# Ranks of scores counted by ScalarE's signs beside VectorE, and three inner products later in their turn

## The chip, the cores and the metric

The kernel runs on one core of one Trainium2 chip. The core has five engines with a queue of instructions each: TensorE (PE in the profile, its weight loads PEld), VectorE (DVE), ScalarE (ACT), GpSimd (POOL) and SyncE (SP), which here only issues DMAs. An engine takes its own instructions strictly in order; between engines there are semaphores. The metric is the device time of one launch in microseconds (us), the median of several runs.

## The reference, cut to what matters

Six layers of a decoder work on x, 16 sequences of 128 tokens by 256 features. Each is followed by a residual and a layernorm: a mixture of experts with ternary weights, a cross attention with a distance bias, an int4 feed-forward layer, **a state-space model with a memory pool**, a masked cross attention, and a feed-forward layer of chosen experts. The change lies in the fourth:

```python
xn = _rmsnorm(x, norm_w)
z, xBC, dt = split(xn @ in_proj_w)            # 512, 512+128+128, 8 columns
dt = softplus(dt + dt_bias)
xBC = silu(conv4(xBC))                        # 4 taps along the tokens
xs, Bm, Cm = split(xBC)
y = _ssd(xs * dt, dt * A, Bm, Cm) + xs * D    # decayed, causal (Cm Bm^T) xs
y = _rmsnorm(y * silu(z), ssm_norm_w) @ out_proj_w
scores = sigmoid(relu(y @ scorer_w1) @ scorer_w2)
summaries = y @ summ_w
# a scan over all 2048 tokens: a token with score > 0.5 is written to one of
# 50 slots; when they are full it replaces the lowest if it is higher
pool, count = scan(step, summaries, scores)
retrieved = softmax(y @ q_w @ (pool @ k_w).T / 4) @ (pool @ v_w)
y = y + sigmoid([y, retrieved] @ gate_w) * retrieved
```

The kernel has no scan. It gives every token a rank: the number of tokens with a higher score, plus the equal ones that came earlier. The 50 tokens with the lowest ranks are the pool.

## The kernel before, in words

One sequence is one block of 128 tokens, on the 128 partitions; there are NB = 16 blocks, n = 0 to 15, in four groups g of four. `stage3` calls `ssm` and then `memory`. Both have a written-out order: in `ssm` the order of the program text is the order on every engine, in `memory` this holds for PE alone. Before that, `stage2` (cross attention, L915 to L1003, and the int4 layer) runs under a scheduler that orders the instructions by need.

`ssm` has a **prologue** for the first group, and then 18 **turns** n = 0 to 17. In turn n the block n is finished, block n+1 is prepared, block n−1 is written back, and two of the six column sets of the next group's convolution are made. The small functions, with their lines and engines:

- `convolved` L1294 (PE, in_proj), `taps` L1296 and L1303 (ACT, DVE: four taps), `tanh` L1309 (ACT) and `curved` L1312 (DVE) make cT, the silu of the convolution, of one column set of a group. Silu is u·(1+tanh u) with u half the argument, so the weights carry a 0.5: L1631 scales the z half of in_proj on DVE, in the prologue.
- `decay` L1387 (POOL) and `decayed` L1392, L1393 (ACT) make the decay matrix mT of a block. `inner(n+1)` L1399 to L1407 makes B·C of the block (PE), masks it (bc, DVE), transposes xs (PE L1404) and scales it by dt (xd, DVE). `joined` L1411 (POOL) multiplies mT by bc.
- `gate` L1423 (PE), `gate_tanh` L1429 (ACT), `gated` L1435 (DVE) make silu(z) for two blocks.
- `outer(n)` L1443 (PE) multiplies mT and xd into ps_y, `skipped` L1452 (DVE) adds xs·D, `passed` L1458 (POOL) multiplies by silu(z): yf.
- `measured` L1463 (ACT, square) and `added` L1469 (POOL) prepare the RMS norm, `projected` L1476 (PE) is out_proj, `summed` L1481 (PE), L1483 (DVE, ys) and L1485 (POOL, yrs) make the factor, `scaled` L1490 (ACT, y) and L1491 (DVE, x), `kept` L1496 (PE) and an ACT copy make yT.
- The norm's weight is multiplied into out_proj once: four instructions L1646 on DVE in the prologue.
- After each group: `remembered(g)` L1504, L1506, L1512, L1513, L1516 and L1520, L1521 (query, summaries, scores of 512 tokens), in turns 7, 11, 13 and after the last. `lined` L1528 and `ranked` L1536 to L1542 bring the scores of the group to all partitions as `row` and to columns as `key`, in turns 8, 12, 14 and after the last.
- `counted(g)` is a generator on DVE: three instructions for equal scores (L1551, L1554, L1555), then for each block b up to 4g+3 one comparison of its 128 keys with the group's 512 row entries (L1560, summed as it goes), and one more with all earlier blocks (L1564) if b is in the group. Two of its steps are taken at the end of every turn from 11 on, and all that is left after the last turn. The sums land in columns of `larger`.
- `others(k)` copies k banks of the fifth layer's keys and values, which PE makes meanwhile (L1905, L1912), out of PSUM (kv, ACT L1583) and stores them (SP, L1584). Each third bank uses the one ps_y buffer.

At the start of `memory` PE makes twelve further parts of the fifth layer's keys and values (`meanwhile(12)`: L1958 and L1978, each copied to a ring by ACT at L1961 and L1982), with two PSUM buffers between them. DVE counts meanwhile, and then reduces `larger` to `rank` (L1758). With `rank`, a matrix `pick` of tokens by slots is made, and PE collects the summaries with it (L1770).

Of the kernel before, what the change touches and what calls it, by code (L numbers as in the profile page):

```python
# [19 lines left out]
P = 128  # L20
NB = 16
# [1201 lines left out]
def stage3(K, w, kv_banks, between):  # L1223

    tc, nc = K.tc, K.nc
    with ExitStack() as ctx:
        keep = ctx.enter_context(tc.tile_pool(name="s3_keep", bufs=1, side="right"))


        m = SimpleNamespace(pool=keep)  # L1230
        m.yT = K.new(keep, [P, KD, NB * P], F32, "yT")
        m.qT = K.new(keep, [SUM, NB * P], F32, "qT")
        m.summ = K.new(keep, [P, NB, SUM], F32, "summ")
        m.score = K.new(keep, [P, NB], F32, "score")
        m.key = K.new(keep, [P, NB], F32, "key")
        m.row = K.new(keep, [P, NB, P], F32, "row")
        m.larger = K.new(keep, [P, 6, NB], F32, "larger")
        nc.vector.memset(m.larger, 0.0)
        ssm(K, w, m, kv_banks)
        memory(K, w, m, between())  # L1240


def ssm(K, w, m, kv_banks):
# [6 lines left out]
    with ExitStack() as ctx:  # L1250
# [178 lines left out]
        def gate_tanh():  # L1429
            to, pz = gates[0]  # L1430
            nc.scalar.activation(to, pz, AF.Tanh)

# [45 lines left out]
        def summed(n):  # L1478
# [3 lines left out]
            t = K.new(small, [P, 1], F32, "ys")  # L1482
            nc.vector.tensor_scalar(t, pn, 1.0 / DI, 1e-5, ALU.mult, ALU.add)  # L1483
            s.yrs = K.new(small, [P, 1], F32, "yrs")
# [15 lines left out]
        def remembered(g):  # L1500
# [19 lines left out]
            nc.scalar.activation(score, psc, AF.Tanh, scale=0.5)  # L1520
            nc.vector.tensor_scalar(score, score, 1.0, 0.5, ALU.add, ALU.mult)  # L1521


        def lined(g):
# [3 lines left out]
            nc.vector.tensor_tensor(  # L1528
                diag, K.ident.unsqueeze(1).to_broadcast(W), m.score[:, mine].unsqueeze(2).to_broadcast(W), ALU.mult,
            )  # L1530

        def ranked(g):
# [6 lines left out]
            pkey = K.new(ps, [P, 4], F32, "ps_s", bufs=1)  # L1539
            nc.tensor.matmul(pkey, K.ident, m.score[:, mine], start=True, stop=True)  # L1540
            nc.scalar.copy(m.row[:, mine, :], prow)
            nc.vector.tensor_copy(m.key[:, mine], pkey)  # L1542

        def counted(g):
            mine = slice(4 * g, 4 * g + 4)
            W = [P, 4, P]
            rowf = m.row.rearrange("p b t -> p (b t)")
            junk = K.new(m.pool, [P, NB * P], BF16, "junk")
            end = 512 * g + 512
            own = junk[:, :512].rearrange("p (b t) -> p b t", t=P)  # L1550
            nc.vector.tensor_tensor(  # L1551
                own, m.row[:, mine, :], m.key[:, mine].unsqueeze(2).to_broadcast(W), ALU.is_equal,
            )
            nc.vector.tensor_tensor(own, own, K.lower.unsqueeze(1).to_broadcast(W), ALU.mult)  # L1554
            nc.vector.tensor_reduce(m.larger[:, 5, mine], own, AX.X, ALU.add)  # L1555
            yield
            for b in range(4 * g + 4):
                s = m.key[:, b:b + 1]
                at = max(b * P, 512 * g)
# [3 lines left out]
                if b >= max(4 * g, 1):  # L1563
# [3 lines left out]
                    )  # L1567
                if b % 4 == 3:
                    yield

# [14 lines left out]


        squared(0)
        normed(0)
# [41 lines left out]
        curved(0, 1)  # L1630
        nc.vector.tensor_scalar(w.inp[:, :, :DI], w.inp[:, :, :DI], 0.5, None, ALU.mult)  # L1631
        taps(0, 2)
# [11 lines left out]
        gate(1)  # L1644
        for k in range(DI // P):
            nc.vector.tensor_scalar(w.out[:, k, :], w.out[:, k, :], w.ssm_norm[:, k:k + 1], None, ALU.mult)  # L1646
        others(2)
        curved(0, 3)
        inner(0)
        joined(0)  # L1650
        order, late, counts = (4, 5, 0, 1, 2, 3), None, iter(())
        for n in range(NB + 2):
# [17 lines left out]
            elif gating:  # L1670
# [3 lines left out]
                gate_tanh()  # L1674
            if late is not None and i == 3:
                curved(*late)
                late = None
            if new:
                inner(n + 1)
            if late is not None:  # L1680
                curved(*late)
            if new:
                decayed(n + 1)
# [14 lines left out]
            if old:  # L1698
                summed(n - 1)
            if n == NB:  # L1700
                others(4)
            if now:
# [14 lines left out]
            if n in (7, 11, 13):  # L1717
                remembered({7: 0, 11: 1, 13: 2}[n])
            if n in (8, 12, 14):
                k = {8: 0, 12: 1, 14: 2}[n]  # L1720
                ranked(k)
                counts = counted(k)
            if n > 10:
                next(counts, None)
                next(counts, None)
        remembered(3)
        all_of(counts)
        lined(3)
        ranked(3)
        all_of(counted(3))  # L1730
        assert next(banks, None) is None and not gates


def memory(K, w, m, kv):
    tc, nc = K.tc, K.nc
    x = K.x
    with ExitStack() as ctx:
# [19 lines left out]
        rank = K.new(one, [P, NB], F32, "rank")  # L1757
        nc.vector.tensor_reduce(rank, m.larger.rearrange("p k b -> p b k"), AX.X, ALU.add)  # L1758
        pick = K.new(one, [P, NB, SLOTS], F32, "pick")
        ppool = K.new(ps, [SUM, SLOTS], F32, "ps_s")  # L1760
# [822 lines left out]
```

## Time and profile before

| | |
|---|---|
| three runs | 1406.60, 1406.64, 1410.62 us; median 1406.64 us |
| the profiled execution | 1407.58 us |
| its span, first to last instruction | 1405.9 us, 1.68 us less |
| mean granted clock of TensorE | 0.950 |
| busy shares | PE 88%, DVE 60%, ACT 47%, POOL 35% |
| prologue of `ssm` | about 410 to 456 us of the span |
| turns 0 to 11 | about 456 to 590 us |
| turns 12 to 17, and the last ranks' row | about 590 to 662 us |
| twelve parts for the fifth layer, beside the last counts | 662 to 685 us |

Times in the text are microseconds from the start of the span. An entry of the timeline is: start, duration, engine, line, what is written from what, shape; in square brackets the idle time before it, and what ended it. A row of a chain has start, duration, engine, tile and line of each step of the work that ended last; a row of waits has what waits, for what, the sum of the waits, how often, and the longest.

### The profile page before, as it was taken

The page shows a single profiled execution, that of the slowest core. Times are in us where ns is not written, and L with a number is a line of the kernel's source. Part 1 is how long each engine was busy: PE and PEld are TensorE (multiplying, and loading weights), DVE is VectorE, ACT ScalarE, POOL GpSimd, SP SyncE. Part 2 cuts the span into 40 slices and gives each one's busy share as a digit, 9 for nine tenths or more (in the row PEclk, how much of TensorE's full clock was granted, in tenths as well). Part 3 has the DMA queues.
Part 4 walks back from the last instruction along what each step waited for, and adds up shares of the span by engine and source line. Part 5 has one row for each costly group of instructions (what it writes and reads, how often), then busy time and mean ns, then how long its engine had stood idle before and what let it go on. Part 6 is the DMA issues. An engine that isn't in the chain of part 4 may idle for free.

```text
span 1405.9 us, 19207 instructions
## 1 busy us (share of the span) xinstructions
PE 1239.4 (88%) x6743; PEld 851.2 (61%) x6743; DVE 842.1 (60%) x1791; ACT 658.1 (47%) x1689; POOL 489.8 (35%) x643
## 2 busy tenths in 40 slices
PE   3678887889978798878998999999889999999995
PEld 1455444667654576655655788877777655666553
DVE  7799978999958887876644565667333111211115
ACT  5779865789955655422223566654522111111110
POOL 4256557678851776641043233222202000000003
PEclk9899988999999999867999999999999999999998
DMA  8458324111112211102000221211005232232002
GB/s 300 143 172 291 120 80 84 17 39 31 32 53 69 72 49 46 45 1 83 8 0 1 69 83 61 76 61 46 1 8 188 69 99 62 85 105 91 21 9 75
DMA packets 63120, 103.53 MB, mean 74 GB/s; under 512 B 11920, under 2 KB 41712, under 8 KB 62768
## 3 DMA queue, kind: packets, MB, share of 16 engines
q1 hardware_dynamic: 60848, 96.76, 20.7%
q0 software_dynamic: 2176, 5.55, 1.9%
q8 instruction: 53, 0.87, 0.3%
q14 instruction: 43, 0.35, 0.1%
HBM read 81.74 MB, written 16.35 MB: 70 GB/s over the span
## 4 chain that ended last, share of the span: by engine, by line
PE 53%; DVE 29%; ACT 6%; POOL 5%; issue 4%; DMA 2%; another core or an unknown queue 0%; SPq 0%; DVEq 0%; POOLq 0%; ACTq 0%
PE ps_y L2413 7%; PE ps_m L2402 7%; PE ps_g L2402 7%; PE ps_m L1958 4%; DVE acc L1303 3%; PE ps_m L2089 3%; PE ps_t L2080 2%; ACT s L2060 2%; DVE cT L1312 2%; PE ps_m L1978 2%; DVE s L915 1%; DVE m L2054 1%; DVE s L2050 1%; PE ps_s L2047 1%; PE ps_t L2069 1%
## 5 line engine op out<-in xcount | busy, mean ns | idle before, releaser
L2407 DVE TENSOR_TENSOR h<-h,ps_m 128x512 f32<-128x512 f32 x60 | 41.3, 688 | 228.3 <-PE ps_m L2402 228.3
L82 POOL TENSOR_SCALAR ln_t<-ln_mv 128x1 f32<-128x1 f32 (+1 forms) x84 | 16.6, 197 | 448.7 <-DVE ln_mv L90 308.3
L2060 ACT ACTIVATE s<-s,m 128x128 f32<-128x128 f32 x256 | 99.4, 390 | 69.1 <-DVE m L2054 69.1
L2406 ACT ACTIVATE h<-ps_g 128x512 f32<-128x512 f32 x60 | 35.8, 597 | 171.0 <-PE ps_g L2402 171.0
L2402 PE MATMUL ps_g<-xin,w 128*128 128x512 f32 x224 | 106.2, 592 | 0.0
L2402 PE MATMUL ps_m<-xin,w 128*128 128x512 f32 x224 | 105.3, 592 | 0.0
L2413 PE MATMUL ps_y<-w,h 128*128 128x256 f32 x448 | 97.8, 379 | 0.0
L2413 PEld LDWEIGHTS ps_y<-w,h 128*128 128x128 f32 x448 | 85.1, 190 | 14.6 <-issue 3.3
L2064 POOL TENSOR_TENSOR s<-s,t 128x1024 f32<-128x1024 f32 x32 | 60.7, 1898 | 90.7 <-DVE t L2063 90.7
L927 ACT ACTIVATE s<-s,m 128x128 f32<-128x128 f32 x256 | 83.2, 394 | 11.7 <-DVE m L922 11.7
L2402 PEld LDWEIGHTS ps_m<-xin,w 128*128 128x128 f32 x224 | 42.5, 190 | 51.4 <-issue 50.2
L2402 PEld LDWEIGHTS ps_g<-xin,w 128*128 128x128 f32 x224 | 42.0, 190 | 46.4 <-issue 45.0
L1958 PE MATMUL ps_m<-xT,half 128*128 128x256 f32 x256 | 62.6, 389 | 2.6 <-DVE qT L1963 1.9
L2050 DVE TENSOR_TENSOR s<-ps_s,hide 128x1024 f32<-128x1024 f32 x32 | 39.2, 1224 | 35.9 <-PE ps_s L2047 35.9
L2414 ACT COPY y<-ps_y 128x256 f32<-128x256 f32 x30 | 11.2, 372 | 104.7 <-PE ps_y L2413 66.2
L2089 PE MATMUL ps_m<-half,oT 128*128 128x256 f32 x256 | 59.3, 385 | 0.0
L1303 DVE SCALAR_TENSOR_TENSOR acc<-ps_m,l1a_conv_w,acc 128x508 f32<-128x508 f32 (+2 forms) x72 | 53.3, 740 | 3.4 <-ACT acc L1296 1.7
L1958 PEld LDWEIGHTS ps_m<-xT,half 128*128 128x128 f32 x256 | 47.4, 194 | 9.2 <-DVE qT L1963 2.3
L2089 PEld LDWEIGHTS ps_m<-half,oT 128*128 128x128 f32 x256 | 47.4, 190 | 7.5
L83 POOL TENSOR_TENSOR ln_rs<-ln_t,mhalf 128x1 f32<-128x1 f32 (+1 forms) x84 | 48.7, 580 | 7.0
L1411 POOL TENSOR_TENSOR mT<-mT,bc 128x1024 f32<-128x1024 f32 x16 | 37.7, 2357 | 36.3 <-DVE bc L1401 16.9
L2060 ACT ACTIVATION_READ_ACCUMULATOR s<-s,m 128x1 f32 x256 | 48.2, 188 | 0.0
(514 smaller groups left out, 3111.2 us busy)
## 6 DMA issues: line engine op xcount, KB each, us to landing
w<-in_w_gate_dram SPq DMA_DIRECT2D x9, 1024.0 KB
csb<-cs_dram SPq DMA_DIRECT2D x16, 512.0 KB
w<-in_l1f_gateT_dram SPq DMA_DIRECT2D x14, 512.0 KB
w<-in_l1f_upT_dram SPq DMA_DIRECT2D x14, 512.0 KB
w<-in_l1f_downT_dram SPq DMA_DIRECT2D x14, 512.0 KB
k<-kv SPq DMA_DIRECT2D x20, 256.0 KB
v<-kv SPq DMA_DIRECT2D x20, 256.0 KB
ring<-k SPq DMA_DIRECT2D x10, 512.0 KB
```

The source lines that it names most:

```text
L83: return self.nc.gpsimd.tensor_tensor(out, t, self.mhalf[: out.shape[0], :n], ALU.pow)
L927: nc.scalar.activation(at, at, AF.Exp, bias=m[h][:, i:i + 1])
L1303: nc.vector.scalar_tensor_tensor(accv[:, :, j:], pcv[:, :, :P - j], w.conv[:, c, TAPS - 1 - j:TAPS - j], accv[:, :, j:], ALU.mult, ALU.add,)
L1411: nc.gpsimd.tensor_tensor(st[n].mT, st[n].mT, bc, ALU.mult)
L1958: nc.tensor.matmul(pq[:, j, :], wt[k][:, at], src[:, k, :], start=(k == 0), stop=(k == KD - 1))
L2050: nc.vector.tensor_tensor(half(b, j), pss.rearrange("p r c k -> p (r c) k"), hide.unsqueeze(1).to_broadcast([P, 8, P]), ALU.add,)
L2060: nc.scalar.activation(at, at, AF.Exp, bias=m[j][:, i:i + 1], accum_out=t[j][:, i:i + 1])
L2064: nc.gpsimd.tensor_tensor(half(b, j), half(b, j), t[j].unsqueeze(2).to_broadcast([P, 8, P]), ALU.mult)
L2089: nc.tensor.matmul(py[b], oT[b][:, c, :], w.o[c // 4][:, c % 4, :], start=(c == 0), stop=(c == NC - 1))
L2402: nc.tensor.matmul(ps[:, j, :], m[k][:, c * P:(c + 1) * P], self.r.xin[:, k, e, cols], start=(k == 0), stop=(k == KD - 1),)
L2407: nc.vector.tensor_tensor(h, h, pu, ALU.mult)
L2413: nc.tensor.matmul(pd, rows(c), w.down[c // 4][:, c % 4, :], start=(c == 0), stop=(c == FI // P - 1))
```

## The change

- **Scalings.** L1631 goes; the gate's tanh halves its input instead (`scale=0.5`). What this leaves, a factor of two in yf, is taken back in `ys` (0.25 for 1) and in out_proj (times 0.5). The four instructions on out_proj go from DVE (L1646) to POOL; they depend only on loaded weights, and stand on POOL's queue in `stage2`, between the two L989 at 329.79 and 330.98. The clearing of `larger` (and of a new `signs`) goes from DVE to POOL, before the prologue.
- **Inner products.** In turns 3, 7 and 11, the last of a group, `inner(n+1)`, `decayed(n+1)` and `joined(n+1)` come after `projected`, `gated` and `summed` of the turn, not before. They use the next group's cT, whose last two `curved` fall into this turn.
- **Banks for the fifth layer.** One bank fewer is copied at the end of the prologue, one each in turns 12, 14 and 15, between `summed` and `outer`, and two instead of four in turn 16.
- **Counts.** Scores are turned into whole units of 2^-24 (`units`, one small DVE instruction per group); row and key are made of these. Two small DVE instructions per group make −key∓0.5, the biases `above` and `below`. A count can then be made by ACT as well: the sign of row + bias, summed as it goes into `signs`; a count is (sum of signs + number)/2, and a POOL instruction of one column adds the half number. The turns change too: turn 11 does group 0 on DVE as before; turn 12 counts nothing (before: equals of group 1 and four blocks); turn 13 equals of group 1, DVE blocks 4 and 5, ACT 0 and 1; turn 14 DVE 6, 7, ACT 2, 3; turn 15 equals of group 2, DVE 8, 9, ACT 0 to 3; turn 16 DVE 10, 11, ACT 4 to 7. For group 3, after the turns, ACT takes blocks 0 to 5, 14 and 15 (ten passes: six of 512 elements, then 256, 1792, 128 and 1920), DVE 6 to 13. These ACT passes stand on ACT's queue ahead of all copies to the ring in `memory`. In `memory` one reduction and one small combination on DVE join `signs` to `rank`.

```diff
-        nc.vector.memset(m.larger, 0.0)
+        m.units, m.below, m.above = (K.new(keep, [P, NB], F32, t) for t in ("units", "below", "above"))
+        m.larger = K.new(keep, [P, 7, NB], F32, "larger")
+        nc.gpsimd.memset(m.larger, 0.0)
+        m.signs = K.new(keep, [P, 5, NB], F32, "signs")
+        nc.gpsimd.memset(m.signs, 0.0)
...
-            nc.scalar.activation(to, pz, AF.Tanh)
+            nc.scalar.activation(to, pz, AF.Tanh, scale=0.5)
...
-            nc.vector.tensor_scalar(t, pn, 1.0 / DI, 1e-5, ALU.mult, ALU.add)
+            nc.vector.tensor_scalar(t, pn, 0.25 / DI, 1e-5, ALU.mult, ALU.add)
...
+            nc.vector.tensor_scalar(m.units[:, 4 * g:4 * g + 4], score, 0.5, 2.0 ** 24, ALU.subtract, ALU.mult)
...
             nc.vector.tensor_copy(m.key[:, mine], pkey)
+            nc.vector.tensor_scalar(m.above[:, mine], m.key[:, mine], -1.0, -0.5, ALU.mult, ALU.add)
+            nc.vector.tensor_scalar(m.below[:, mine], m.key[:, mine], -1.0, 0.5, ALU.mult, ALU.add)
...
+            def by_scalar(b):
+                junk = held["junk"]
+                at = max(b * P, 512 * g)
+                nc.scalar.activation(
+                    junk[:, at:end], rowf[:, at:end], AF.Sign, bias=m.above[:, b:b + 1],
+                    accum_out=m.signs[:, g, b:b + 1],
+                )
+                n = end - at
+                if b >= max(4 * g, 1):
+                    nc.scalar.activation(
+                        junk[:, :b * P], rowf[:, :b * P], AF.Sign, bias=m.below[:, b:b + 1],
+                        accum_out=m.signs[:, 4, b:b + 1],
+                    )
+                    n += b * P
+                nc.gpsimd.tensor_scalar(m.larger[:, 6, b:b + 1], m.larger[:, 6, b:b + 1], 0.5 * n, None, ALU.add)
...
+        for k in range(DI // P):
+            nc.gpsimd.tensor_scalar(w.out[:, k, :], w.out[:, k, :], w.ssm_norm[:, k:k + 1], 0.5, ALU.mult, ALU.mult)
...
-        nc.vector.tensor_scalar(w.inp[:, :, :DI], w.inp[:, :, :DI], 0.5, None, ALU.mult)
...
-        for k in range(DI // P):
-            nc.vector.tensor_scalar(w.out[:, k, :], w.out[:, k, :], w.ssm_norm[:, k:k + 1], None, ALU.mult)
-        others(2)
+        others(1)
...
+        counts = {
+            11: ((equals0, None), (vector0, 0, 1, 2, 3)), 13: ((equals1, None), (vector1, 4, 5), (scalar1, 0, 1)),
+            14: ((vector1, 6, 7), (scalar1, 2, 3)), 15: ((equals2, None), (vector2, 8, 9), (scalar2, 0, 1, 2, 3)),
+            16: ((vector2, 10, 11), (scalar2, 4, 5, 6, 7)),
+        }
...
-            if late is not None and i == 3:
-                curved(*late)
-                late = None
-            if new:
+            if new and i < 3:
                 inner(n + 1)
             if late is not None:
                 curved(*late)
-            if new:
+            if new and i < 3:
                 decayed(n + 1)
                 joined(n + 1)
...
+            if new and i == 3:
+                inner(n + 1)
+                decayed(n + 1)
+                joined(n + 1)
+            if n in (12, 14, 15):
+                others(1)
             if n == NB:
-                others(4)
+                others(2)
...
+        for k in range(8):
+            by_scalar((0, 1, 2, 3, 4, 5, 14, 15)[k])
+            by_vector((6, 7, 8, 9, 10, 11, 12, 13)[k])
...
+        signs = K.new(one, [P, NB], F32, "signs_all")
+        nc.vector.tensor_reduce(signs, m.signs.rearrange("p k b -> p b k"), AX.X, ALU.add)
+        nc.vector.scalar_tensor_tensor(rank, signs, 0.5, rank, ALU.mult, ALU.add)
```

## The prediction

> **What bounds the kernel now.** I read the page first, for the shares of the chain that ended last. It stands for the whole span.
>
> ```profile
> span 1405.9 us, 19207 instructions
> PE 53%; DVE 29%; ACT 6%; POOL 5%; issue 4%; DMA 2%; another core or an unknown queue 0%; SPq 0%; DVEq 0%; POOLq 0%; ACTq 0%
> ```
>
> The change touches some 250 us of it, the state-space layer. So I cut that into stages by windows (columns: bounds, length, busy time of PE, PEld, DVE, ACT, POOL with counts, granted clock of PE, DMA).
>
> ```profile
> 410.00:456.00 46.00, 40.78 (x151) 24.29 (x152) 32.23 (x73) 27.70 (x66) 7.79 (x11) 0.93 0.18 64
> 456.00:590.00 134.00, 117.63 (x645) 86.44 (x644) 107.48 (x198) 77.28 (x125) 93.03 (x73) 0.96 0.17 58
> 590.00:662.00 72.00, 55.24 (x223) 37.61 (x224) 48.85 (x120) 17.92 (x35) 24.52 (x22) 0.74 0.04 15
> 662.00:690.00 28.00, 27.49 (x125) 19.73 (x125) 23.68 (x55) 7.63 (x13) 0.00 (x0) 0.94 0.23 76
> ```
>
> The turns to 590 are PE's, at nearly full clock. From 590 to 662 nothing is full and the clock is 0.74: there waits decide. From 662 PE is full; DVE counts below it. The waits of PE between 415 and 665, and the timeline of turn 3, say where PE stands still.
>
> ```profile
> PE ps_m L1404 <- DVE cT L1312: 12.4, 4, 4.2
> PE ps_s L1481 <- DVE bc L1401: 5.2, 3, 2.2
> ```
>
> ```profile
> 489.70 1.59 POOL L1469 TENSOR_TENSOR sq<-sq 128x256 f32<-128x256 f32 x2
> 491.02 0.33 PE L1404 MATMUL ps_m<-ident,cT 128*128 128x128 f32 x1 [4.21 <-DVE cT L1312]
> 491.19 3.50 PE L1476 MATMUL ps_o<-l1a_out_proj,yf 128*128 128x256 f32 x8
> 494.82 1.09 PE L1443 MATMUL ps_y<-mT,xd 128*64 128x128 f32 x16
> 497.16 1.27 POOL L1458 TENSOR_TENSOR yf<-yf,sz 128x512 f32<-128x512 f32 x1 [1.45 <-DVE yf L1452]
> ```
>
> PE waits 4.21 us for the last curved set, and then out_proj's eight matmuls take 3.50 us, where at full clock the same eight take 1.89. The chain of waits has them in all three turns, and in turn 13 the products after the fourth group's scores:
>
> ```profile
> 454.05 1.05 DVE l1a_out_proj L1646 x4
> 491.35 3.33 PE ps_o L1476 x8
> 532.06 3.08 PE ps_o L1476 x8
> 575.91 2.58 PE ps_o L1476 x8
> 608.30 3.78 PE ps_m L1504 x4
> 661.80 8.94 PE ps_m L1958 x32
> ```
>
> **The change part by part.** Base is the profiled execution, 1407.58 us (span 1405.9 and 1.68 around it), 0.94 above the median 1406.64.
>
> *Stage 2, POOL.* Four products of 128x256 on POOL before L989 at 330.98. They read one large input. The nearest rows are a POOL memset (L823, 128x2560 in 2.22 us, so 0.22 for 256 columns, 0.35 with some 0.13 of start, an estimate from L82's 0.19 for one column) and L989, two inputs of the same shape, 0.73. Four: 1.4 to 2.9, I take the middle, 2.2. Their weights landed near 328.3, before POOL is there (330.5), so no DMA is waited for. POOL had 0.46 idle there; behind stands L989, L935 and the factor ln_rs at 334.95, which DVE took at 335.63, 0.7 later. So 2.2−0.46−0.7 = **+1.1** (0 to +2.4); DVE is busy 14.35 of the 15 us from 325 to 340 and may be late enough itself to hide it all, hence the 0; +2.4 is the upper price, 2.9, with the idle alone taken off. The two memsets lie in an idle of POOL of 2.4 us: 0.
>
> *Prologue.* DVE's chain loses L1631 (0.60) and L1646 (1.05), 1.65. Curved(0,3) at 455.02 then waits for its tanh, done at 454.2: it can start 1.4 to 1.5 earlier. **−1.5** (−1.3 to −1.65). One bank less there (ACT 0.59, a store of SP): ACT is 60% busy, 0.
>
> *Turns 3, 7, 11.* L1476 moves into the idle before 491.02: its yf is there at 487.9, it ends about 489.8 at the full clock that PE still has. What is late next is POOL's sq, at 491.29, for L1481. Then L1399, L1404 and L1443, about 492.5 in place of 494.82; yf on DVE 493.7. But POOL is behind too: ys and yrs, then L1411 (bc now later, 2.34) ends at about 495.05; L1458 behind it starts there, for 497.16: −2.1. Turn 7: 537.81 to 535.75. Turn 11: L1504 from 580.61 to 578.5. **−6.3** (0 to −6.6; three sums of 2.1). DVE had 2.25 idle before ys in turn 3, so it can follow; 0 is the end where the next turns are DVE's (80% busy) and not PE's.
>
> *Turn 12.* 6.77 us of counts (597.41 to 604.18) leave DVE ahead of bc(14). bc was waited for by PE's L1481 (part of the 5.2 us) and POOL's L1411 (2.97). Next late are PE's gate products and the tanh (sz), mT's Exp on ACT to 603.27, then L1411, yrs, y, yT, L1504, which stood at 608.30 and comes at 605.6 to 607.0: **−2.0** (−1.0 to −2.7).
>
> *Clock in turn 13.* L1504, L1512 and L1516 took 8.9 us at clock 0.50 (608.30 to 617.2); in turn 11 the three took 4.6 at full clock (580.61 to 585.2), after the turns 6.4 (651.47 to 657.86) at 0.73 to 0.79. PE idled 1.60 and 1.94 just before, and both waits shrink, so I take the row in the middle: 8.9−6.4 = **−2.5** (0 to −4.3).
>
> *Turns 13 to 17.* DVE loses group 1's and 2's blocks to ACT: two, two, four and four passes. An ACT pass of 512 is 0.62 (L1463, the same shape) plus its accumulator read of 0.19, less overlap: 0.72. In turns 15 and 16 four each, 2.9, stand ahead of sq(15) and yT(15) on ACT's queue, and a bank's copy (0.59) ahead of outer(15), which needs ps_y: PE's L1912 (2.00) and the copy put +1.65 there; SP's store is behind it and nobody waits for that. Against it: ys in turn 16 came behind DVE's counts at 646.66, and two banks fewer stand there. Row by row 34.35 in place of 34.05 from the third scores to L1504 of the last group: **+0.3** (−1.5 to +2.5). Units and biases, three DVE instructions of 0.15 per group, on the chain in the last: **+0.2** (0 to +0.5). POOL's columns of 0.2 stand behind nothing that is late.
>
> *Last ranks.* After the row copy (661.16 to 661.75) ACT has ten passes: six of 0.72, then 0.50, 1.82, 0.39, 1.93 (0.86 ns an element, from L1392's 128x1024 of 1.05, and 0.18): 8.95 (7.95 to 10.8). Counted from the row copy's start, they run from 0.75 to 9.7. Only then ACT copies PE's first finished part, till 10.3. A part is eight matmuls of L1958, 1.73 each in the later four (6.91) and 3.8 for the first of the early four (8.94−3×1.73). PE has two PSUM buffers: it does two parts, from 0.64 to 6.15, and waits for that copy, 4.15 us idle. Ten parts at 1.72 are left, till 27.5; after 4.21 us of idle in turn 3 eight matmuls were 1.6 slow, here the first part was 2.0 slow, so 1.8 more: 29.3, where L1770 stood at 23.86 (685.02−661.16). **+5.5** (+2.7, cheap passes and no half clock, to +7.7, dear passes). DVE's counts fall from 20 to 10 us there, and that is worth 0: they lay beside PE's parts, which end at 684.5. What the parts cost PE is the same, so nothing behind them is shorter.
>
> Sum: +1.1−1.5−6.3−2.0−2.5+0.3+0.2+5.5 = **−5.2**, so 1402.4 as a profiled execution, and 0.94 less, 1401.4, as a median.
>
> A rule of the Trainium skill speaks against the tail. "TensorE: Matmul & The Clock Gate", Part 1, says that the clock is halved after one idle window of about 3.4 us and comes back after about 3.4 us of sustained work. Turn 3 agrees (4.21 us idle, then 3.50 for 1.89). Turn 13 does not quite: the rows show 0.50 from 608 to 620 with PE busy 3.7 to 4.0 of every 4. By the page alone the tail's second idle costs about 1.7, an estimate, near the 1.8 that I took from the row; by turn 13's row the whole tail could run at half.
>
> **The rivals.**
>
> R1, slower: after its idle PE stays at half clock, as from 608 to 620. A part at half is +1.8. The sum holds one; with 6 more the change is −5.2+10.8 = +5.6, and from there R1 decides; all nine give +11.0, 1417.6. For it: turn 13. Against it: before, the parts began at 0.50 and were at 0.62 within two, 0.94 over the stage; PE is dense there.
>
> R2, the move does nothing: turns 4 and 8 start no earlier, since POOL (L1411, L1387, 93 of 134 us) or DVE carries them. −5.2+6.3 = +1.1: 1407.7, no change. For it: L1411 is later than before against L1399. Against: PE's 117.6 of 134 is the fullest, and DVE has 4.6 us idle in turn 3 in four pieces.
>
> R3, better: full clock in turn 13 (−1.8 more), POOL's products hidden in stage 2 (−1.1), the passes at 7.95 and no half clock after them (−2.0): −10.1, 1396.5. For it: clock 1.00 after 646.
>
> R4, stage 2 loses more: POOL's delay goes round between DVE and POOL once more, +2 to +3: 1403.9, no change. For it: DVE's 14.35 of 15 us there. Against: later idles of POOL.
>
> **How the numbers follow.** A change under 0.3%, 4.2 us, is about what a measurement of this kernel cannot tell from none; faster begins below 1402.4. The main case has 0.44 and its own range 1398.5 to 1404.7, from the half clock in turn 13 and the passes; 0.27 of it falls under 1402.4 and 0.17 over it. R3 0.20, faster. R2 0.13 and R4 0.08, same. R1 0.10, slower; 0.05 for ACT's passes holding up turns 15 and 16 by more than their bound, slower. Faster 0.47, same 0.38, slower 0.15. The range 1394 to 1410 leaves out R1 and the last case, and 0.05 below it.
>
> **What would show it.** Right: L1476 in turns 3, 7 and 11 at 1.9 us, and PE waiting there for POOL's sq; L1443 at 492.5 less the prologue's gain; no DVE count between turns 12's L1491 and bc; ten ACT passes after the last row copy, then a wait of PE on ACT of about 4 us at the third part, and DVE idle long before L1770. Wrong: turns 4 and 8 starting their L1443 no earlier than before, once the prologue's gain is taken off (R2); PE's clock at 0.5 for 10 us in the parts (R1); a sign pass far from 0.72, or a load of ACT's table beside it; PE waiting for yT(15) in turn 17 for more than 3 us.

## The result, and the profile after

In the first comparison the changed kernel took 1408.13 us (median of 20 runs, 1402.73 to 1412.90), the kernel before 1407.93 us (20 runs, 1405.85 to 1410.62): ratio 0.9998, 95% interval 0.9987 to 1.0009. In absolute terms that is between 1.8 us less and 1.3 us more. The change made no difference that this measurement can tell; 1401.4 us was forecast, 5.2 less than before. The profiled execution took 1408.86 us.

To find where the 5.2 us went I cut both profiled executions at the same events, read off the timeline: the 11th, 16th and 32nd row of stage 2's x (L1003), the yf of blocks 2 and 11 (L1458, now L1461), the third group's scores (L1521, now L1524), the last row copy (L1541, now L1546), the start of the sum over slots (L1770, now L1810), the first x row that the fourth layer's layernorm writes behind it (L93, near 710 us), and the end of the last output row. Each number is the us from one event to the next.

| stretch | before | after | difference | forecast for it |
|---|---|---|---|---|
| start to x row 11 of stage 2 | 327.08 | 328.97 | +1.9 | 0, nothing changed there |
| x row 11 to 16, GpSimd's four products | 21.56 | 22.75 | +1.2 | +1.1 |
| x row 16 to 32 | 63.01 | 63.02 | 0.0 | 0 |
| to yf(2): prologue, first turns | 74.96 | 72.62 | −2.3 | −1.5 |
| to yf(11): turns 3 to 11 | 95.05 | 91.01 | −4.0 | −6.3 |
| to the third scores: turns 12, 13 | 35.76 | 31.70 | −4.1 | −4.5 |
| to the last row copy: turns 14 to 17 | 43.74 | 45.50 | +1.8 | +0.5 |
| to the sum over slots: last ranks | 23.86 | 31.45 | +7.6 | +5.5 |
| to x at 710 | 24.69 | 23.16 | −1.5 | 0 |
| to the end of the last output row | 693.35 | 694.09 | +0.7 | 0 |

The stretches from row 11 to 710 add up to −1.4 us. The first and last rows hold none of the change; a profile of the same changed kernel taken later has 331.06 in the first. So single stretches, which repeat within some 0.1 us where TensorE's clock does the same, say more than one profile's total.

The page and the windows of the same four stages, of the changed kernel, answer to those shown of before:

```profile
span 1407.2 us, 19229 instructions
...
PE 52%; DVE 29%; ACT 8%; POOL 6%; issue 4%; DMA 1%; another core or an unknown queue 0%; SPq 0%; DVEq 0%; ACTq 0%; POOLq 0%
```

```profile
410.00:456.00 46.00, 39.25 (x151) 23.31 (x151) 32.04 (x71) 26.58 (x65) 9.38 (x16) 0.96 0.19 59
456.00:590.00 134.00, 119.23 (x650) 85.19 (x651) 111.75 (x214) 78.14 (x127) 94.47 (x74) 0.97 0.16 54
590.00:662.00 72.00, 52.85 (x239) 33.64 (x237) 43.16 (x102) 33.06 (x75) 26.62 (x42) 0.83 0.08 26
662.00:690.00 28.00, 23.43 (x99) 16.65 (x100) 9.09 (x23) 10.84 (x18) 0.00 (x0) 0.88 0.23 75
```

From 590 to 662 VectorE is busy 43.16 us and not 48.85, ScalarE 33.06 and not 17.92, and TensorE's clock is 0.83 and not 0.74. These windows stand at the same microseconds in both kernels, though, and the changed kernel makes its last row copy at 655.57 and not at 661.16, so 6.4 us of its last ranks lie in the third window. From that copy to the sum over slots the windows are, of the kernel before and then of the changed one:

```profile
661.16:685.02 23.86, 22.89 (x81) 16.46 (x82) 23.16 (x52) 7.51 (x13) 0.00 (x0) 0.91 0.27 89
```

```profile
655.57:687.02 31.45, 25.74 (x82) 18.24 (x82) 14.82 (x36) 16.46 (x32) 0.00 (x0) 0.84 0.20 67
```

The change did what it says: VectorE's work falls from 23.16 to 14.82 us and ScalarE's rises from 7.51 to 16.46. But TensorE, which fills the stretch, now stands still for 5.7 us and not 1.0. In the chain ScalarE has 8% and not 6. Where TensorE stands still is in its waits, here of the changed kernel from 415 to 690 (what waits, for what, sum, times, longest):

```profile
PE ps_o L1479 <- POOL yf L1461: 10.1, 9, 2.3
PE ps_m L1507 <- ACT yT L1500: 6.0, 2, 3.1
PE ps_s L1484 <- DVE bc L1404: 5.7, 2, 3.0
PE ps_s L1484 <- POOL sq L1472: 5.6, 6, 1.4
PE ps_m L1998 <- ACT ring L2001: 5.3, 1, 5.3
PE ps_m L1407 <- DVE cT L1315: 2.0, 1, 2.0
```

The waits for the last curved set in turns 3, 7 and 11 (11.9 of the 12.4 us before) are gone, as intended; the one of 2.0 that is left lies in the prologue. The waits for yf (7.2 us before) and for sq are what replaced them. Those for yT are one of 2.9 in turn 13 and one of 3.1 in turn 17, and the wait for the ring copy is the stop of the last ranks. The timeline of the changed kernel shows the last ranks:

```profile
655.57 0.59 ACT L1546 COPY row<-ps_m 128x512 f32<-128x512 f32 x1 [3.30 <-PE ps_m L1541]
...
656.18 0.72 ACT L1582 ACTIVATE csb<-row,above 128x512 bf16<-128x512 f32 x1
...
657.03 0.72 ACT L1582 ACTIVATE csb<-row,above 128x512 bf16<-128x512 f32 x1
...
663.93 1.88 ACT L1588 ACTIVATE csb<-row,below 128x1920 bf16<-128x1920 f32 x1
...
665.93 1.07 ACT L2001 COPY ring<-ps_m 128x512 f32<-128x512 f32 x2
...
666.57 6.74 PE L1998 MATMUL ps_m<-ctxT,l1x_W_k 128*128 128x256 f32 x16 [5.25 <-ACT ring L2001]
...
673.15 7.03 PE L2018 MATMUL ps_m<-l1x_W_v,ctxT 128*128 128x512 f32 x16
...
687.02 2.07 PE L1810 MATMUL ps_s<-pick,summ 128*64 128x50 f32 x32
```

The passes follow each other every 0.85 us, the first ring copy stands behind all ten, PE waits 5.25 us for it, and then needs 6.74 us for two parts (16 matmuls) that take 3.5 at full clock. The windows of the changed kernel have the clock in the column before the DMA share:

```profile
662.00:666.00 4.00, 0.00 (x0) 0.00 (x0) 3.89 (x9) 3.97 (x7) 0.00 (x0) 0.99 0.00 0
666.00:672.00 6.00, 5.43 (x13) 4.35 (x14) 4.99 (x14) 1.59 (x3) 0.00 (x0) 0.50 0.85 282
672.00:687.00 15.00, 15.00 (x53) 9.85 (x51) 0.00 (x0) 4.69 (x8) 0.00 (x0) 0.98 0.08 27
```

Four microseconds without a matmul (the wait began at 661.3), 6.8 at half clock, then full clock. The trace also records each change of the granted clock. In the 17 traces of this case it is 1.00 or 0.50 and nothing else, and the time between two changes is 3.41 us or a whole multiple of it; here it was 0.50 from 665.9 to 672.7. A mean such as 0.74 is a mixture of the two. Below, a stay is such a time at half clock.

### The profile page after: what moved, and what is told of

Read it like the earlier page. It is cut to its first block, busy times and chain, and to the rows that moved or that the text cites. A ratio compares the mean times of both kernels' runs of the same rounds, so it can differ in the third digit from the quotient of the medians.

```text
span 1407.2 us, 19229 instructions
## 1 busy us (share of the span) xinstructions
PE 1234.8 (88%) x6731; PEld 843.2 (60%) x6743; DVE 824.7 (59%) x1755; ACT 676.4 (48%) x1733; POOL 495.5 (35%) x669
## 4 chain that ended last, share of the span: by engine, by line
PE 52%; DVE 29%; ACT 8%; POOL 6%; issue 4%; DMA 1%; another core or an unknown queue 0%; SPq 0%; DVEq 0%; ACTq 0%; POOLq 0%
PE ps_y L2453 7%; PE ps_m L2442 7%; PE ps_g L2442 7%; PE ps_m L1998 4%; DVE acc L1306 2%; PE ps_m L2129 2%; ACT s L2100 2%; PE ps_t L2120 2%; PE ps_m L2018 2%; DVE cT L1315 1%; DVE s L915 1%; DVE m L2094 1%; DVE s L2090 1%; PE ps_t L2109 1%; PE ps_s L2087 1%
## 5 line engine op out<-in xcount | busy, mean ns | idle before, releaser
L927 ACT ACTIVATE s<-s,m 128x128 f32<-128x128 f32 x256 | 83.3, 395 | 11.7 <-DVE m L922 11.7
```

The source lines that it names most:

```text
L927: nc.scalar.activation(at, at, AF.Exp, bias=m[h][:, i:i + 1])
```

## The experiments

Every run is set against runs of the kernel before on the same chip, whose median was 1406.8, 1408.5, 1407.1 and 1404.5 us in the four groups of runs. So ratios are compared, not microseconds: 0.001 is 1.4 us. A ratio below is to the kernel before, with its 95% interval; the changed kernel's own is 0.9998. The stretches of the table above, taken in the profiles of ten of these runs:

| kernel | prologue | turns 3-11 | turns 12, 13 | turns 14-17 | last ranks | to 710 |
|---|---|---|---|---|---|---|
| before | 74.96 | 95.05 | 35.76 | 43.74 | 23.86 | 24.69 |
| changed | 72.62 | 91.01 | 31.70 | 45.50 | 31.45 | 23.16 |
| counts on VectorE | 72.00 | 92.58 | 34.52 | 48.29 | 24.82 | 26.42 |
| four passes | 72.67 | 90.99 | 31.68 | 45.49 | 22.90 | 24.80 |
| copies between | 71.92 | 92.41 | 29.11 | 44.05 | 23.29 | 24.75 |
| yT first | 72.62 | 90.95 | 33.29 | 39.50 | 30.12 | 24.80 |
| both repairs, second time | 71.90 | 92.21 | 33.30 | 39.53 | 23.42 | 24.82 |
| move undone | 71.85 | 95.62 | 31.66 | 48.28 | 30.01 | 24.75 |
| move undone, second time | 72.97 | 95.05 | 32.08 | 43.93 | 30.12 | 24.75 |
| before, with the move | 73.91 | 91.31 | 34.71 | 43.65 | 23.86 | 24.70 |

A stretch has the same number in many kernels and jumps by 1 to 3 us in others, where nothing of it was edited (turns 14 to 17 with the counts on VectorE: 48.29 and not 45.50, in the same order). Each of these jumps that I followed up was TensorE at half clock for a few microseconds more or less. So one profile shows where a wait is; what it is worth needs many runs.

### The changed kernel again

> The changed kernel as it is, beside the others of this row on one chip, so that each can be set against it and not only against the kernel before. Every theory: ratio 0.999 to 1.002 to the kernel before, as in the first comparison; the sum of slots starts 31.4 us after the last row copy's start.

1407.95 us, ratio 0.9997 (0.9980 to 1.0014). All its stretches from row 11 to 710 agree with the first profile within 0.02 us. The comparison holds.

### Last ranks: all counts on VectorE

```diff
-        for k in range(8):
-            by_scalar((0, 1, 2, 3, 4, 5, 14, 15)[k])
-            by_vector((6, 7, 8, 9, 10, 11, 12, 13)[k])
+        for b in range(NB):
+            by_vector(b)
```

> The changed kernel with all sixteen blocks of the last group counted by VectorE again, as before; the turns' sign passes stay. Theory (ScalarE's ten passes ahead of the ring copies stop TensorE): the profile of the changed kernel has the sum of slots start 31.45 us after the last row copy's start, against 23.86 before, 7.6 more, and 1.5 of it come back by 709 us. Without the passes: 23.9 again, no wait of TensorE on the ring copy, and 1408.1 - 7.6 + 1.5 = 1402.0 us (1400.5 to 1403.5). Rival (the stall only takes the place of half-clock time that comes anyway, or stands in this one profile alone): 1407 to 1409.

1404.81 us, ratio 0.9975 (0.9953 to 0.9997): less than the changed kernel, by about half of what was expected. PE's wait for the ring copy is gone and the last ranks take 24.82 us. But 3.3 us come back behind them (26.42 for 23.16). The timeline of this version, PE:

```profile
675.70 7.07 PE L1997 MATMUL ps_m<-ctxT,l1x_W_k 128*128 128x256 f32 x32
684.33 2.04 PE L1809 MATMUL ps_s<-pick,summ 128*64 128x50 f32 x32 [1.56 <-issue]
...
689.30 5.58 PE L1850 MATMUL ps_m<-kkT,qT 64*128 64x50 f32 x32
```

VectorE with all sixteen blocks is done later than PE's parts, and PE stands still for 1.56 us. Behind it the products of queries and keys take 5.58 us, where the changed kernel needs 3.73 for the same 32. The windows from the sum over slots to x at 710, of this version and then of the changed kernel, have clocks of 0.81 and 0.93:

```profile
684.33:710.75 26.42, 26.42 (x113) 15.58 (x114) 8.08 (x24) 5.54 (x12) 1.49 (x3) 0.81 0.00 1
```

```profile
687.02:710.18 23.16, 23.16 (x114) 13.35 (x114) 7.69 (x22) 6.13 (x13) 1.49 (x3) 0.93 0.00 1
```

PE is busy throughout in both. In the record of the clock the stays there are 10.2 and 3.4 us; half of the difference is 3.4, which is what came back. That the stop of 1.56 us made the longer stay is likely but not shown, since the next version has no stop and still 6.8 us of it.

### Last ranks: four passes on ScalarE

```diff
-        for k in range(8):
-            by_scalar((0, 1, 2, 3, 4, 5, 14, 15)[k])
-            by_vector((6, 7, 8, 9, 10, 11, 12, 13)[k])
+        for k in range(4):
+            by_scalar(k)
+            for b in range(4 + 3 * k, 7 + 3 * k):
+                by_vector(b)
```

> The changed kernel, but of the last group ScalarE takes only blocks 0 to 3 (four passes of 512 elements, 0.85 us apart) and VectorE the other twelve. Theory (TensorE stops because the ring copies stand behind 9.7 us of passes, and its clock falls in the stop): four passes end 4.0 us after the row copy's start, before TensorE has its two parts done (5.1 to 6.2), so no wait on the ring copy, the sum of slots 23.5 to 24 us after the row copy's start in place of 31.45, and, since VectorE is done before TensorE, TensorE stays dense to the next products and they cost 23.2 us to 710 as in the changed kernel, not 26.4 as with all counts on VectorE: 7.5 us less than the changed kernel, 1400.5 us. Rival (any ScalarE pass beside TensorE's parts costs, in proportion): 4/10 of 7.6 remain, 1403.5 us. Rival (what the tail gains comes back after it, as 3.2 of 6.6 did with all counts on VectorE): 1404.5 us.

1399.17 us, ratio 0.9943 (0.9928 to 0.9958), 7.7 us less than the changed kernel by the ratios. That meets the theory; the rivals' 1403.5 and 1404.5 fall. The timeline of this version shows PE going on without a stop, and the slots' sum 22.90 us after the row copy:

```profile
653.62 0.59 ACT L1546 COPY row<-ps_m 128x512 f32<-128x512 f32 x1 [3.30 <-PE ps_m L1541]
...
654.26 8.56 PE L1999 MATMUL ps_m<-ctxT,l1x_W_k 128*128 128x256 f32 x32 [0.46 <-ACT row L1546]
...
657.72 0.59 ACT L2002 COPY ring<-ps_m 128x512 f32<-128x512 f32 x1
...
662.65 7.03 PE L2019 MATMUL ps_m<-l1x_W_v,ctxT 128*128 128x512 f32 x16
...
676.52 2.07 PE L1811 MATMUL ps_s<-pick,summ 128*64 128x50 f32 x32
```

One part of the expectation fell: the stretch behind took 24.80 and not 23.2, although PE was dense. Its window:

```profile
676.52:701.32 24.80, 24.80 (x114) 14.28 (x114) 7.70 (x23) 6.12 (x13) 1.48 (x3) 0.86 0.00 1
```

With the clock at 1.00 or 0.50, a mean of 0.86 over 24.80 us is 6.9 us at half clock; the record has 6.8. So the three values of this stretch in all the profiles, 23.2, 24.7 to 24.8 and 26.4, are the same work with 3.4, 6.8 and 10.2 us at half clock. What sets the length of the stay I can't say.

### Last ranks: ten passes, copies in between

The sign passes are issued in `memory`, one block after each part, and write to a tile of that function.

```diff
-        meanwhile(12)
+        for b in (0, 1, 2, 3, 4, 5, 14, 15):
+            meanwhile(1)
+            m.by_scalar(b)
+        meanwhile(4)
```

> The changed kernel with the same ten sign passes of the last group on ScalarE, but the copies to the ring in between them: three passes, a copy, two passes, a copy, a pass, a copy and so on. TensorE's order is the same. Theory (the order on ScalarE's queue makes the stop, not the passes): TensorE waits for a copy at most some 1.5 us, behind a long pass; the sum of slots 23 to 25 us after the row copy's start in place of 31.45; some 7 us less than the changed kernel, 1401 us, ratio to the kernel before 0.995. Rival (ScalarE's passes slow TensorE's parts as such): 28 us and more, 1405.

The stretch answers: 23.29 us with all ten passes and their full length, as against 31.45; TensorE's order was the same. It waits for no ring copy. It is the place on ScalarE's queue and not the passes. The time moved less than the theory said: 1401.77 us, ratio 0.9984 (0.9968 to 0.9999), where 0.995 was expected. On this chip the kernel before took 1404.5 us, 2 to 4 us less than elsewhere. Between row 11 and 710 this version's one profile adds up to 3.0 us less than that of the version with four passes. What is longer in it is the start to row 11, 331.52 for 327.02 us, where the two kernels do the same. Whether the missing time lies there in the other executions too, the record doesn't show.

### TensorE kept at work in the stop

```diff
-        meanwhile(12)
+        meanwhile(2)
+        spin = K.new(ps, [P, 512], F32, "ps_s")
+        for _ in range(10):
+            nc.tensor.matmul(spin, K.ones, m.row[:, :4, :].rearrange("p b t -> p (b t)"), start=True, stop=True)
+        meanwhile(10)
```

> The changed kernel with ten products of ones by the scores' row, used by nobody, on TensorE between the second and third of its parts, so that it works through the 5.25 us in which it waits for ScalarE's passes. Nothing else moves. Theory (the wait costs 5.25 by itself, and 2.3 more since the clock falls after it: two parts at 3.4 us in place of 1.72): the wait is filled, the third part starts at the same time, but at full clock; the sum of slots 28 to 29 us after the row copy's start in place of 31.45, 1405 us. Rival (the slow parts have another reason, data or the DMA of 356 GB/s beside them): 31.4, 1408.

The filler was too long: its ten products became 20 matmuls and 8.75 us, 3.5 more than the stop. So the time says nothing (1409.48 us, ratio 1.0030, 1.0009 to 1.0051). But the timeline of this version answers the question, since the two parts behind the filler run at full clock:

```profile
661.52 8.75 PE L1794 MATMUL ps_s<-row,ones 128*128 128x512 f32 x20
670.10 3.62 PE L2002 MATMUL ps_m<-ctxT,l1x_W_k 128*128 128x256 f32 x16
```

3.62 us where the changed kernel took 6.74, beside the same loads (352 GB/s of DMA from 670.1 to 673.6, and 313 in the changed kernel from 666.57 to 673.15): the clock cost 3.1 us on top of the stop's 5.25. The rival (data, or the DMA) falls.

### The sign passes of turn 16 behind the last yT

```diff
-            16: ((vector2, 10, 11), (scalar2, 4, 5, 6, 7)),
+            16: ((vector2, 10, 11),), 17: ((scalar2, 4, 5, 6, 7),),
```

> The changed kernel with the four sign passes of turn 16 one turn later on ScalarE's queue, behind the copy of the last block's yT. In the profile of the changed kernel the passes stand ahead of that copy, from 642.29 to 645.55, and TensorE waits 3.07 us for it and then runs the last group's query product at 3.4 us in place of 1.9. Theory (this wait is the 1.5 us that turns 14 to 17 lost): the copy 2.7 us earlier, the passes hidden in ScalarE's idle 4.2 us behind it, 1 to 1.5 more from the clock: 1404 us (1403 to 1406). Rival (TensorE waits for something else there, or loses the same by the clock): 1408.

1398.92 us, ratio 0.9938 (0.9922 to 0.9953): more than was expected. The timelines, the changed kernel first:

```profile
642.29 0.72 ACT L1582 ACTIVATE csb<-row,above 128x512 bf16<-128x512 f32 x1
...
645.55 0.35 ACT L1500 COPY yT<-ps_o 128x256 f32<-128x256 f32 x1
```

```profile
643.89 0.37 ACT L1500 COPY yT<-ps_o 128x256 f32<-128x256 f32 x1 [0.53 <-PE ps_o L1499]
...
644.16 0.72 ACT L1582 ACTIVATE csb<-row,above 128x512 bf16<-128x512 f32 x1
644.31 1.98 PE L1507 MATMUL ps_m<-yT,l1a_qw 128*128 128x512 f32 x4 [0.46 <-ACT yT L1500]
```

In the changed kernel four passes run between the two copies of yT, PE waits 3.07 us, and the query product behind it takes 3.39 us. In this version the copy comes first, PE waits 0.46, the product takes 1.98, and the passes run beside it for nothing. Turns 14 to 17 take 39.50 us and not 45.50, 6.0 less: about 3 of the wait, the rest of the clock. But turns 12 and 13, which are as in the changed kernel, take 1.6 more in this profile, since their stay of 6.8 us became one of 13.6 that reaches into turn 14. From turn 12 to 17 the five profiles with this order take 71.3 to 73.3 us, and the ten with the changed kernel's order 76.0 to 82.8, but for 73.2 in the version with copies between. So 4 to 5 us is a surer figure for the order than 6. The rival falls. From row 11 to 710 this profile is only 4.3 us shorter than the changed kernel's, and the time 8.4 by the ratios; the rest of that I can't place.

### Both repairs

> Both edits, the late passes of turn 16 and four passes in the last group. Theory: the sum, 1408.1 - 7.5 - 3.5 = 1397 us (1395.5 to 1399.5), ratio to the kernel before 0.992. Rival (a dense stretch moves the half clock to the next products): 1401 to 1404.

> The version with the late passes of turn 16 and four passes in the last group once more, for more runs. Theory: the stretches that it changes add up to 14.1 us less than before, ratio 0.989 to 0.990. Rival (the four runs were lucky, the neighbours with one more edit had 0.9925 and 0.9947): 0.992 to 0.993.

Four runs gave 1391.61 us, ratio 0.9881 (0.9865 to 0.9898), six on another chip 1395.33 us, ratio 0.9919 (0.9896 to 0.9943). The two intervals just overlap. The profile of the first has 31.96 and not 33.30 us in turns 12 and 13 and 23.18 and not 24.82 behind the last ranks, the lower of two values that both stretches have in other kernels too. From row 11 to 710 the two profiles take 14.1 and 11.7 us less than the kernel before. By the two medians this version is 11 to 17 us faster than the kernel before, and it beats both kernels.

### The move in turns 3, 7 and 11

Undone in the changed kernel, twice; undone in the version with both repairs; and done alone in the kernel before:

```diff
-            if new and i < 3:
+            if late is not None and i == 3:
+                curved(*late)
+                late = None
+            if new:
                 inner(n + 1)
...
-            if new and i == 3:
-                inner(n + 1)
-                decayed(n + 1)
-                joined(n + 1)
```

> The changed kernel with the inner products, the decay and the join of turns 3, 7 and 11 back ahead of out_proj. Theory (the move is worth what the profile shows, 1.9, 0.3 and 1.85 us from turn 2 to turn 11): 1408.1 + 4.0 = 1412.1 us (1411 to 1413.5), TensorE waits some 4.2 us for the last curved set three times, and out_proj behind it takes 2.7 to 3.5 us in place of 1.99. Rival (the turns are bound by GpSimd and VectorE, the order on TensorE is worth nothing): 1408.1.

> The changed kernel with the move in turns 3, 7 and 11 undone, once more. Theory (the move is worth 4 us, as in the kernel before, where it alone gave 0.9959): ratio to the kernel before 1.0025 to 1.003. Rival (in the changed kernel it is worth nothing): 0.9995.

> The version with late passes in turn 16 and four passes in the last group, with the inner products of turns 3, 7 and 11 back ahead of out_proj. Theory (the move is worth what the profiles with and without it differ by, 95.0 against 91.0 us from turn 2 to turn 11): 1391.6 + 4.3 = 1396 us, ratio to the kernel before 0.991. Rival (worth nothing in the time, since the undone move changed the median of the changed kernel by only -0.0 to -1.5 us): 1391.6, ratio 0.988.

> The kernel before with the later inner products of turns 3, 7 and 11 as its only change. Theory: 4.0 us from turn 2 to turn 11, 1404 us, ratio 0.997. Rival (worth nothing, later turns or the clock take it): 1408, ratio 1.000.

| kernel | ratio | turns 3-11 |
|---|---|---|
| changed, move undone | 0.9994 (0.9972 to 1.0016) | 95.62 |
| the same, second time | 1.0016 (0.9995 to 1.0037) | 95.05 |
| both repairs, move undone | 0.9947 (0.9926 to 0.9968), with it 0.9881 and 0.9919 | 95.62 |
| before, with the move | 0.9959 (0.9941 to 0.9976) | 91.31 |

The profiles agree: 91 to 92.6 us with the move, 95 to 95.6 without. In the kernel before, and with both repairs, the time follows, with 5.8 us and 4 to 9 us. In the changed kernel it does not clearly: −0.6 and +2.5 us by the ratios, each ±3. The theory's +4 lies outside the first interval and inside the second. So the move is worth about 4 us in its own turns, and the rival (nothing) falls with the kernel before. Most of the 4 us is clock: in these turns TensorE is at half clock for 3.4 us in the changed kernel and 10.2 in the kernel before, and for 10.2 or 13.7 in the three profiles with the move undone.

Why undoing it costs the changed kernel less is open in part. In both of those profiles the last ranks took 30.0 or 30.1 and not 31.45. In the first of them the time from 710 to the end of the span, where nothing was edited, is 691.67 us with 18.8 at half clock, for 696.97 with 34.7 in the changed kernel, and in that execution it takes back the cost; in the second it is 697.17. The kernel before with the move has such a short end too, 691.23 for 696.17 us, so its 5.8 us are not all the move's.

### GpSimd's products in the prologue, or on ScalarE

> The changed kernel with GpSimd's four products on out_proj moved out of stage 2 into the prologue of the state-space model, behind the normalisation factors. Theory (they delay stage 2): of the 2.8 us that stage 2 lost in the profile, 1.2 came at the products (from +1.89 at 330 to +3.08 at 349) and 1.6 ahead of them, near 298, which the products can't have made. So stage 2 gets 1.2 back, the prologue has room on GpSimd (8 of 46 us busy), 1406.9 us. Rival A (all 2.8 is theirs): 1405.3. Rival B (VectorE hides them, the shift is the run's): 1408.1.

1410.07 us, ratio 1.0023 (1.0010 to 1.0036), worse, against all three forecasts. Stage 2 got its 1.19 us back (21.56 for 22.75), and the prologue lost 1.9 (74.50 for 72.62). The timeline of this version:

```profile
418.85 1.14 DVE L1276 TENSOR_SCALAR csb<-x,rs 128x256 f32<-128x256 f32 x4 [2.91 <-POOL rs L83]
...
421.13 1.93 POOL L1645 TENSOR_SCALAR l1a_out_proj<-l1a_out_proj,l1a_ssm_norm_w 128x256 f32<-128x256 f32 x4
421.17 2.04 DVE L1276 TENSOR_SCALAR csb<-x,rs 128x256 f32<-128x256 f32 x4 [0.52 <-POOL rs L83]
```

The same four instructions on DVE take 1.14 us alone and 2.04 beside GpSimd's products, and they are on the chain of the prologue. That is 0.9; the other 0.9 is 16 matmuls ahead of it at a lower clock. An idle engine was no free place. The loss of 3.5 us against the changed kernel is not explained by this: from row 11 to 710 the profile is 1.0 us longer, and the profiled execution, 1403.49 us, was the shortest of the twelve. With the counts on VectorE as well:

> Both of the first two edits: last group's counts on VectorE, GpSimd's products in the prologue. Theory: 1402.0 - 1.2 = 1400.8 us (1399.5 to 1402.5), the sum of the two gains, since the places lie 300 us apart. Rival (the clock takes back what one place gives): 1405 to 1408.

1404.49 us, ratio 0.9974 (0.9949 to 0.9999), no better than the counts on VectorE alone: this edit gave nothing here. On ScalarE ahead of turn 0, on top of both repairs (`nc.scalar.mul` of each quarter by the halved weight):

> The version with late passes in turn 16 and four passes in the last group, and the four products on out_proj on ScalarE ahead of turn 0 in place of GpSimd in stage 2 (GpSimd halves the small weight vector in the prologue). Theory (GpSimd's products cost 1.2 us in stage 2, the same 1.19 in every profile with them, and ScalarE, idle for 2.7 of 4 us at the start of turn 0, makes them for nothing): 1391.6 - 1.2 = 1390.4 us; the stretch of stage 2 behind them 21.56 us and not 22.75, the prologue to turn 2 unchanged within 0.5. Rival (no room there either, as on GpSimd in the prologue, where it cost 1.9): 1391.6 to 1392.5.

1395.04 us, ratio 0.9925 (0.9899 to 0.9952). The products' stretch is 21.56 again, but rows 16 to 32 took 63.93 and not 63.02, the prologue 73.02 and not 71.9, and the whole is not faster than without it. What the 1.2 us are worth can't be told with so few runs.

## Why the prediction was wrong

The forecast was 1401.4 us, faster by 5.2; the change measured nothing, between −1.8 and +1.3 us, a case to which it gave 0.38 in all. From row 11 to 710 the two profiles differ by −1.4 us where the sum had −5.2; the rest of the difference lies in parts that were not edited. The signs of the terms were right. Four sizes were not.

- **Last ranks, +5.5 forecast, +7.6 in the profile.** The mechanism was right: ten passes ahead of the ring copies, two PSUM buffers, a stop of PE, half clock after it. Two numbers were too small. A pass of 512 with its read comes every 0.85 us, not 0.72: 0.72 is the pass alone, and the read of 0.19 hides only 0.06 of itself, so ten passes took 9.7 us (656.18 to 665.90) and not 8.95, and the stop 5.25 and not 4.15. And two parts ran at half clock, not one: 3.1 us by the filler's run, not 1.8. R1 was the case of more such parts; it needed six and there was one. The wait and the order were shown by the versions with four passes and with copies between, the clock by the filler.
- **Turns 3, 7 and 11, −6.3 forecast, −4.0 in the profile.** Turns 3 and 11 gave 1.9 each, near the 2.1. PE waits for POOL's sq there, 1.41 us, as forecast. In each of the two a stay of 3.4 us at half clock (491.3 to 494.7 and 576.7 to 580.1 before) is gone, which is worth up to 1.7. Turn 7 gave 1.35 and lost 1.05 of it in turn 8. Its stay remained (532.3 to 535.7 before, 532.8 to 536.2 after): the clock fell there also without the long wait. The windows of turn 7, of the kernel before and then of the changed one:

```profile
532.00:536.00 4.00, 4.00 (x21) 3.33 (x21) 1.44 (x3) 1.28 (x2) 2.61 (x2) 0.57 0.27 96
```

```profile
532.00:536.00 4.00, 4.00 (x25) 2.66 (x24) 2.50 (x7) 1.01 (x3) 3.17 (x3) 0.60 0.04 15
```

  The slow microseconds only hit other matmuls: out_proj runs in 1.99 and not 3.25, but outer takes 1.67 and not 1.27 and the query product 2.73 and not 1.88. My step "it ends at the full clock that PE still has" held for L1476 and was not asked for what follows. R2 named turns 4 and 8 as the place where the gain could vanish; of turn 8 that was so, but for the clock and not for POOL or DVE.
- **Turns 14 to 17, +0.5 forecast, +1.8.** The four passes ahead of yT(15) were priced as 2.9 us beside other work and set off against VectorE's shorter counts. They stood on the path: PE waited 3.07 us and then had half clock. Taking that order away gave 6.0 us in that stretch of one profile, and 4 to 5 with turns 12 and 13 counted in. PE's wait for bc in turn 14 also grew, from 1.42 to 3.00 us, behind the counts of turn 13 on VectorE. The whole came to only +1.8; TensorE was at half clock for 13.6 us of this stretch and not for 19.8, which the sum had not counted. That a wait of more than 3 us in turn 17 would show the prediction wrong was written down, and it was there.
- **Behind the last ranks, 0 forecast, −1.5.** In the changed kernel the stay in the small products was 3.4 us and not 6.8 (23.16 and not 24.69). In most other versions, with the stop or without, it was 6.8 again (24.8).

Right were GpSimd's products (+1.19 against +1.1) and that VectorE's shorter tail is worth almost nothing: PE's last wait there was 0.51 us in the kernel before. Turns 12 and 13 came to −4.1 against −4.5, in part by luck. Turn 12 gave 2.5 for 2.0 by the chain that was forecast, but some of it because the gate's products ran at full clock, 1.97 us for 3.76, which was not in the sum. The products behind the third scores gave 1.6 for 2.5. The reason given for those, that both waits ahead of them shrink, held for one alone: PE's wait for yT grew from 1.94 to 2.88 us, and yet the stay was 6.8 us and not 13.6. Other versions with the same order had 29.1 to 34.5 us in these two turns, for 31.70 here. The prologue gave 2.3 for 1.5; other versions with the same prologue gave 2.0 to 3.1, so a size of 0.8 can't be read from one profile. Small slips of the sum: 2.2−0.46−0.7 is 1.04 and not 1.1, 29.3−23.86 is 5.44 and not 5.5, and the dear passes of 10.8 would have made +7.3 and not +7.7 of it. The worst of the sum was to take the clock for a matter of each stop's length.

A rule had been weighed. "TensorE: Matmul & The Clock Gate" of the Trainium skill, Part 1, has the clock halved after an idle window of about 3.4 us that runs freely, and full again after as long at work. The stop of 5.25 us agrees, and the stays of 3.41 us and its multiples agree with such a window. The work behind the stop ran at half clock from 666.57 to 672.7, 6.1 us, which is more than the page's 3.4. In turn 7 the single waits were 1.67 and 1.41 us and the clock fell to 0.60 all the same, which the page's limit by itself does not give.

## What to carry to other kernels

Before work is given to an idle engine, read what stands behind it on that engine's queue: ten passes ahead of the copies that free two PSUM buffers cost 7.6 us, the same ten with the copies in between cost nothing in that stretch (23.29 us, before 23.86). The same holds for the last link of a chain, here one copy of 0.35 us behind four passes. And where TensorE stands still, price the slow matmuls after the stop as well as the stop, two parts and not one; where it already runs thin, a shorter wait may only move the slow ones.

## What the runs showed of the hardware

- The granted clock of TensorE changed in steps of time: in all 17 traces it was 1.00 or 0.50, and each stay between two changes was 3.41 us or a whole multiple. So a stretch in which matmuls fill every microsecond took 23.2, 24.8 or 26.4 us, with 3.4, 6.8 or 10.2 us at half clock.
- The clock fell without a long stop: in turn 7 after waits of 1.67 and 1.41 us (mean 0.60 from 532 to 536), and in the changed kernel from 696.6 to 700.0, where matmuls filled 23.16 of 23.16 us, behind some 70 products of only 50 columns.
- Four scalings on VectorE went from 1.14 to 2.04 us while GpSimd made four products of the same shape.
- Stretches that no edit touched differ between executions: the start of the program to stage 2's eleventh row took 322.9 to 331.5 us in the profiles here, and the time from 710 to the end of the span 691.2 to 697.2, with 18 to 35 us at half clock. Either is more than the whole change was forecast to bring.
